# Causal attention in a three-part block: the turned softmax weights kept in two buffers, and the large tiles turned in one block at a turn's end

## The chip, the cores and the metric

The kernel runs on one core of a Trainium2 chip. The metric is the device time of one execution in microseconds, as the median of several runs. The core's engines are TensorE (PE; its weight loads are listed as PEld), VectorE (DVE), ScalarE (ACT), GpSimd (POOL) and SyncE (SP), which issues the DMA transfers of this kernel. They run side by side and wait for one another through semaphores.

## The reference

A block of three steps on x of shape (16, 512, 256), all in float32: a feed-forward step that goes by way of slots, causal self-attention with 16 heads of 64, and the feed-forward step again. Only the middle one is touched:

```
b, s, e = x.shape
q = x @ Wq + bq
kv = x @ Wkv + bkv
k, v = jnp.split(kv, [H * DQK], axis=-1)
q = _rope(q.reshape(b, s, H, DQK).transpose(0, 2, 1, 3))
k = _rope(k.reshape(b, s, H, DQK).transpose(0, 2, 1, 3))
v = v.reshape(b, s, H, DV).transpose(0, 2, 1, 3)
scores = jnp.einsum('bhqd,bhkd->bhqk', q, k) * (1.0 / np.sqrt(DQK))
causal = jnp.tril(jnp.ones((s, s), dtype=bool))
scores = jnp.where(causal[None, None], scores, -jnp.inf)
probs = jax.nn.softmax(scores, axis=-1)
out = jnp.einsum('bhqk,bhkd->bqhd', probs, v)
out = out.transpose(0, 2, 1, 3).reshape(b, s, H * DV)
return out @ Wo + bo
```

Here b = 16, s = 512, e = 256, H = 16, DQK = DV = 64; the input of this step is the layer-normalized x, and its result is added to x.

## The kernel before

The attention step is one loop. A unit is a batch and a group of four heads (HG = 4, NHG = 4 groups), so there are 16 x 4 = 64 units, and one turn of the loop works on several units at once: for u it makes the sums of unit u, turns the weights of unit u+1 (`old`), makes the scores of unit u+2 (`new`) and the queries and keys of unit u+3. The order on every engine is the order in which the program is written (manual schedule), SP's queue included.

A unit's scores are a lower triangle of 4 x 4 blocks of 128 x 128 for each head. Tile i holds the queries i*128 to i*128+127, and its keys reach as far as block i: i+1 blocks. The steps for one unit:

- `scores` (L1029): TensorE multiplies queries and keys, two contraction halves of 32 rows, four heads in different row groups of the array, into a PSUM bank per head. Tiles 3 and 2 have four banks each, tiles 1 and 0 share four. There are eight banks in all, taken in rotation.
- `exps`: VectorE scales, masks and takes the row's least value in one custom instruction (L1047), ScalarE makes the exponential and its row sum (L1051). They land in `pr0` (tiles 3 and 2: seven blocks a head) and `pr1` (tiles 1 and 0: three blocks).
- `scaled`: VectorE takes the reciprocal of the row sums (L1056), GpSimd multiplies every row (L1059).
- The sums need keys on the partitions, so every 128 x 128 block has to be turned. `turn` (L1074) is VectorE's transposition within 32 x 32 squares, from pr into `sq`; `turn_most(j)` turns six of the seven blocks of a head of pr0, `turn_corner` the seventh of all four heads, `turn_tile(1)` two blocks of all heads of pr1, `turn_tile(0)` the last one. `move` (L1101) then takes the squares to their places with 16 DMA transfers from sq into `prT`, each of 32 partitions; SP issues them.
- `sums` (L1132): TensorE multiplies the turned weights by the values, for each of two pairs of heads and each key block t over the n = 4 - t tiles that see it, the two heads of a pair in different column groups. ScalarE takes the result out and adds the bias (L1139, into `oT`).
- `leave` (L1148): TensorE's output projection; VectorE adds it to x (L1154), and at a batch's last group the rows are stored (L1156).

There is one sq and one prT (tiles in a pool with one buffer each). In the turn for u VectorE turns the first head of unit u+2 at the end (`turn_most(0)`), after the scores of tiles 1 and 0; the rest of it comes one turn later, after the exponentials of tiles 1 and 0, when the unit is `old`.

Once for each batch, layer-normalized activations also go by way of memory: `Trip` turns squares on VectorE and stores them (`away`, L947), and `land` brings them back in two halves of eight transfers each (`ahT`, L953), one half in each of the two turns that follow. In SP's order a turn is: land's eight transfers if there are any, the move, then away and the two stores of out if there are any.

The first unit and the last one are turned by TensorE instead (`turn_at_once`, L1114). The order around the change, in one turn:

```
                elif old:
                    old.scaled((1, 0), slice(0, HG // 2))
                    old.turn_most(1)
                    old.turn_most(2)
                    old.scaled((1, 0), slice(HG // 2, HG))
                    old.turn_most(3)
                    old.turn_corner()
                    old.turn_tile(1)
                if new:
                    new.scores((3,))
                    new.scores((2,))
                    new.exps((3,), slice(0, 1))
                if old and 0 <= u < nu - 2:
                    old.turn_tile(0)
                    old.move()
```

Of the kernel before, what the change touches and what calls it, by code (L numbers as in the profile page):

```python
# [9 lines left out]
F32 = mybir.dt.float32  # L10
# [24 lines left out]
HG = 4  # L35
# [12 lines left out]
def macaron_kernel(ctx: ExitStack, tc: tile.TileContext, a: dict, out: bass.AP):  # L48
# [840 lines left out]
    def attention(qp, wq, wk, wv, wo, cos, sin, row):  # L889
# [111 lines left out]
        blocks = NT * (NT + 1) // 2  # L1001
        first = [0, 4, 8, 7]
        place = {0: (1, 0, 1), 1: (1, 1, 2), 2: (0, 0, 3), 3: (0, 3, 4)}

        class Weights:
# [3 lines left out]
            def __init__(self, u):  # L1009
# [4 lines left out]
                self.pr = [None, None]  # L1014
# [47 lines left out]
            def turn(self, which, heads, of, src, dst):  # L1062
# [3 lines left out]
                if heads[0] == 0 and which == 0 and len(of) == 2:  # L1066
                    self.sq = ap.tile([P, NSQ, HG, blocks * SQ], F32, tag="sq", name=f"sq{self.nm}")
                pr = self.pr[which]

                def view(x, at, dims):  # L1070
                    return bass.AP(x.tensor, x.offset + at, [list(x.ap[0])] + [[s, n] for s, n in dims if n > 1])
                j, nh = heads
                step = (7, 3)[which] * P
                nc.vector.transpose(  # L1074
                    view(self.sq, j * blocks * SQ + dst[0] * SQ,
                         [(blocks * SQ, nh)] + [(s * SQ, n) for s, (_, n) in zip(dst[1:], of)]
                         + [(HG * blocks * SQ, NSQ), (1, SQ)]),
# [3 lines left out]
            def turn_most(self, j):  # L1081
                self.turn(0, (j, 1), [(3, 2), (1, 3)], 0, (2, 1, 3))

            def turn_corner(self):
                self.turn(0, (0, HG), [], 6, (first[3],))

            def turn_tile(self, i):
                if i:
                    self.turn(1, (0, HG), [(1, 2)], 1, (1, 3))
                else:  # L1090
                    self.turn(1, (0, HG), [], 0, (0,))

            def move(self):
# [3 lines left out]
                prT = prTs[self.u] = ap.tile([P, NSQ, HG, blocks * SQ], F32, tag="prT", name=f"prT{self.nm}")  # L1097
                for n in range(NSQ):
                    for k in range(NSQ):
                        q = (k + n) % NSQ  # L1100
                        nc.sync.dma_start(prT[k * SQ:(k + 1) * SQ, q, :, :], self.sq[q * SQ:(q + 1) * SQ, k, :, :])  # L1101

            def turn_at_once(self, tag, vector):


                prT = prTs[self.u] = ap.tile([P, NSQ, HG, blocks * SQ], F32, tag=tag, name=f"prT{self.nm}")
                where = {first[t] + i - t: (i, t) for i in range(NT) for t in range(i + 1)}
                per = S // P
                for g in range(HG * blocks // per):
                    pt = ps(f"p_prT{self.nm}_{g}")  # L1110
                    for n in range(per):
                        j, at = divmod(g * per + n, blocks)
                        i, t = where[at]
# [215 lines left out]
```

## Time and profile before

| | |
|---|---|
| time, median of 3 runs | 2311.39 us (2309.87 to 2312.6) |
| span of the profiled execution | 2307.9 us |
| granted TensorE clock, mean | 0.998 |
| PE, PEld busy | 98%, 63% |
| DVE, ACT, POOL busy | 76%, 49%, 46% |
| attention loop's sums (L1132), first to last start | 441.8 to 1917.4 us |
| prT<-sq transfers | 992 of 160.0 KB |

The span is the time from the first to the last instruction of one execution under the hardware profiler; the runs' time has what lies around it too. "Busy" is the time in which an engine had an instruction under way, as a share of the span. A share is a mean over stages: in four turns of the loop (1174.8 to 1267.8 us) the stretch-by-stretch view gives PE 92.88 of 93.00 us, DVE 83.69, ACT 50.53 and POOL 55.48. In lists of groups, "out<-in" names the tiles, "xN" is the number of instructions (a float32 product counts as two), then busy time in us, mean ns of one, and the idle time before the group with what ended it. The time of an SP row is that of issuing transfers, not of moving the data.

### The profile page before, as it was taken

What the parts mean: (1) busy time and instruction counts of PE and PEld (TensorE: products, weight loads), DVE (VectorE), ACT (ScalarE), POOL (GpSimd) and SP (SyncE); (2) the same over time, 40 slices, a digit from 0 to 9 for tenths busy, and PEclk for the clock granted to TensorE, in tenths of its full rate; (3) what the DMA queues carried; (4) which work ended last, traced back from release to release, by engine and by line L of the source; (5) the groups of instructions that cost most, each with busy time, mean ns of one, the idle gap of its engine ahead of it and who ended that gap; (6) DMA issues with size and microseconds to landing.
All of it is one profiled execution on the core that took longest, in us unless ns stands there. A gap on an engine that the chain in (4) does not pass through costs nothing. (4 is left out here: it accounts for less than half of the span.)

```text
span 2307.9 us, 42376 instructions
## 1 busy us (share of the span) xinstructions
PE 2253.5 (98%) x14424; PEld 1445.6 (63%) x14424; DVE 1761.7 (76%) x4678; ACT 1122.4 (49%) x3040; POOL 1068.0 (46%) x1692
## 2 busy tenths in 40 slices
PE   7999999999999999999999999999999999998999
PEld 5664588566656556566666665555666666764588
DVE  6742398889889898889898988988888875532387
ACT  6743243555454555455454545455545455542233
POOL 2210053555656566565655565656656552210043
PEclk9999999999999999999999999999999999999999
DMA  7839851145546465555555554646555553839834
GB/s 237 243 129 407 319 138 52 30 109 133 142 105 158 96 158 121 130 131 120 137 132 125 129 142 108 157 97 154 125 127 134 119 120 112 238 127 406 315 117 140
DMA packets 221888, 358.85 MB, mean 155 GB/s; under 512 B 99877, under 2 KB 159849, under 8 KB 213481
## 3 DMA queue, kind: packets, MB, share of 16 engines
q1 hardware_dynamic: 220812, 355.34, 55.9%
q8 instruction: 115, 1.88, 0.3%
q14 instruction: 101, 0.82, 0.1%
q10 hardware_dynamic: 860, 0.81, 0.1%
HBM read 156.29 MB, written 37.22 MB: 84 GB/s over the span
## 5 line engine op out<-in xcount | busy, mean ns | idle before, releaser
L1059 POOL TENSOR_SCALAR pr<-pr,ars 128x512 f32<-128x512 f32 (+3 forms) x1024 | 524.1, 532 | 577.5 <-DVE ars L1056 576.0
L1051 ACT ACTIVATE pr<-pr,amn 128x512 f32<-128x512 f32 (+3 forms) x1024 | 561.6, 550 | 257.4 <-DVE amn L1047 252.9
L1074 DVE STREAM_TRANSPOSE sq<-pr 128x768 f32<-128x768 f32 x434 | 384.6, 918 | 131.4 <-DMA prT<-sq 94.5
L1047 DVE CUSTOM_DVE_ANT_0 pr<-p_as,causal 128x512 f32<-128x512 f32 (+3 forms) x1024 | 433.9, 480 | 8.4 <-PE p_as L1029 7.5
L1029 PE MATMUL p_as<-k,q 32*128 32x512 f32 (+3 forms) x4096 | 315.3, 441 | 0.8 <-ACT aoT L1139 0.8
L996 ACT COPY v<-p_v 128x512 f32<-128x512 f32 x128 | 74.8, 586 | 451.2 <-PE p_v L993 451.2
L1132 PE MATMUL p_av<-prT,v 128*64 128x512 f32 (+3 forms) x2048 | 289.8, 435 | 4.2 <-ACT pr L1051 2.2
L1029 PEld LDWEIGHTS p_as<-k,q 32*128 32x128 f32 x4096 | 188.7, 185 | 108.9 <-issue 74.1
L1148 PE MATMUL p_ay<-wo,aoT 128*128 128x256 f32 x1024 | 240.1, 387 | 11.3 <-DVE amn L1047 9.8
L1148 PEld LDWEIGHTS p_ay<-wo,aoT 128*128 128x128 f32 x1024 | 190.3, 191 | 73.5 <-DVE amn L1047 49.2
L993 PE MATMUL p_v<-wv,ahT 128*128 128x256 f32 x1024 | 231.6, 379 | 0.7 <-DVE x L1154 0.7
L1132 PEld LDWEIGHTS p_av<-prT,v 128*64 128x64 f32 x2048 | 139.6, 137 | 147.6 <-issue 110.7
L971 PE MATMUL p_q<-ahT,wq 128*128 128x512 f32 x512 | 230.6, 593 | 0.2 <-ACT ahT L932 0.2
L971 PE MATMUL p_k<-ahT,wk 128*128 128x512 f32 x512 | 230.3, 592 | 0.0
L993 PEld LDWEIGHTS p_v<-wv,ahT 128*128 128x128 f32 x1024 | 194.5, 190 | 53.8 <-issue 22.2
L1051 ACT ACTIVATION_READ_ACCUMULATOR pr<-pr,amn 128x1 f32 x1024 | 191.6, 187 | 0.0
L971 PEld LDWEIGHTS p_k<-ahT,wk 128*128 128x128 f32 x512 | 97.3, 190 | 122.0 <-issue 106.9
L971 PEld LDWEIGHTS p_q<-ahT,wq 128*128 128x128 f32 x512 | 97.0, 190 | 95.7 <-issue 76.3
L762 POOL TENSOR_TENSOR kbd<-kT,own 128x256 f32<-128x256 f32 x32 | 19.7, 619 | 272.0 <-DVE kT L720 240.4
L815 PE MATMUL p_cy<-vw,catT 128*128 128x256 f32 x512 | 120.8, 379 | 0.0
L588 PE MATMUL p_ds<-hT,qk 128*128 128x512 f32 x256 | 116.0, 596 | 2.1 <-ACT hT L159 2.1
L403 PE MATMUL p_cq<-hT,c_Wq 128*128 128x512 f32 x256 | 115.1, 592 | 0.0
(174 smaller groups left out, 3206.8 us busy)
## 6 DMA issues: line engine op xcount, KB each, us to landing
prT<-sq SPq DMA_DIRECT2D x992, 160.0 KB
w<-in_e_W_dram SPq DMA_DIRECT2D x64, 1024.0 KB
w<-in_e_Wg_dram SPq DMA_DIRECT2D x32, 1024.0 KB
out_dram<-x SPq DMA_DIRECT2D x64, 256.0 KB
awaya<-sqa SPq DMA_DIRECT2D x25, 512.0 KB
atT<-awaya SPq DMA_DIRECT2D x100, 128.0 KB
xl<-in_attn_x_dram SPq DMA_DIRECT2D x16, 512.0 KB
xl<-out_dram SPq DMA_DIRECT2D x16, 512.0 KB
```

Source lines behind the costliest of these rows:

```text
L403: nc.tensor.matmul(pq, w["c_Wq"][:, k, c * P:(c + 1) * P], hTs[b][:, k, :], start=(k == 0), stop=(k == NC - 1))
L588: nc.tensor.matmul(psc, qk[:, k, c * P:(c + 1) * P], hT[:, k, :], start=(k == 0), stop=(k == NC - 1))
L815: nc.tensor.matmul(py[:, t * D:(t + 1) * D], atT[:, c, t * P:(t + 1) * P], vws[b][:, c, :], start=(c == 0), stop=(c == NC - 1))
L971: nc.tensor.matmul(pq, self.w[:, k, at:at + P], hTs[self.b][:, k, :], start=(k == 0), stop=(k == NC - 1))
L993: nc.tensor.matmul(pv[:, t * 256:(t + 1) * 256], hTs[b][:, k, (t0 + t) * P:(t0 + t + 1) * P], wv[:, k, hg * HG * DQ:(hg + 1) * HG * DQ], s ...
L1029: nc.tensor.matmul(banks[j][:, at:at + w], q[n][j * 32:(j + 1) * 32, i * P:(i + 1) * P], k[n][j * 32:(j + 1) * 32, :w], start=(n == 0), st ...
L1047: nc.vector.tensor_tensor_reduce(out=self.at(i, j), in0=banks[j][:, at:at + w], in1=causal[:, S - w:], scale=-1.0 / math.sqrt(DQ), scalar= ...
L1051: nc.scalar.activation(self.at(i, j), self.at(i, j), AF.Exp, bias=self.mn[:, i, j:j + 1], scale=-1.0, accum_out=self.rs[:, i, j:j + 1])
L1059: nc.gpsimd.tensor_scalar(self.at(i, j), self.at(i, j), self.rs[:, i, j:j + 1], 1.0, ALU.mult, ALU.mult)
L1074: nc.vector.transpose(view(self.sq, j * blocks * SQ + dst[0] * SQ, [(blocks * SQ, nh)] + [(s * SQ, n) for s, (_, n) in zip(dst[1:], of)] + ...
L1132: nc.tensor.matmul(po[j * DQ:(j + 1) * DQ, :].rearrange("d (a f) -> d a f", a=NSQ)[:, :, t * SQ:], vs[u][:, t, head * DQ:(head + 1) * DQ], ...
L1148: nc.tensor.matmul(py[:, t * D:(t + 1) * D], oTs[u][:, pair, (t0 + t) * P:(t0 + t + 1) * P], wo[:, hg * (HG // 2) + pair, :], start=(pair ...
```

## The change

Tiles 3 and 2 (index 0) and tiles 1 and 0 (index 1) now have buffers of their own: sq0 and prT0 with seven blocks a head, sq1 and prT1 with three. `where` lists the order of the blocks in each. A move has become two: `move(0)` stands at the start of a turn, `move(1)` after the small tiles have been turned, and each issues 16 transfers, of 112 KB and of 48 KB. All five transpositions of pr0 now stand at the end of the turn in which the unit is `new`, behind the scores of tiles 1 and 0 and ahead of their exponentials; the two of pr1 stay in the next turn, behind the exponentials of two heads of tile 3. `sums` runs over six pieces a pair instead of four, first four from prT0 and then two from prT1: (key block, first tile, tiles) are (0, 2, 2), (1, 2, 2), (2, 2, 2), (3, 3, 1), then (0, 0, 2), (1, 1, 1). `turn_at_once` fills both buffers. The scores and the exponentials are made as before.

```diff
--- before.py
+++ after.py
@@ -998,9 +998,11 @@
 
 
 
-        blocks = NT * (NT + 1) // 2
-        first = [0, 4, 8, 7]
+        blocks = (7, 3)
         place = {0: (1, 0, 1), 1: (1, 1, 2), 2: (0, 0, 3), 3: (0, 3, 4)}
+
+        where = ([(2, 0), (3, 0), (2, 1), (3, 1), (2, 2), (3, 2), (3, 3)], [(0, 0), (1, 0), (1, 1)])
+        pieces = [(0, t, max(t, 2), NT - max(t, 2)) for t in range(NT)] + [(1, t, t, 2 - t) for t in range(2)]
 
         class Weights:
 
@@ -1011,7 +1013,7 @@
                 self.u, self.hg, self.nm = u, hg, f"{b}_{hg}"
                 self.mn = small.tile([P, NT, HG], F32, tag="amn", name=f"amn{self.nm}")
                 self.rs = small.tile([P, NT, HG], F32, tag="ars", name=f"ars{self.nm}")
-                self.pr = [None, None]
+                self.pr, self.sq = [None, None], [None, None]
                 self.banks = {}
 
             def at(self, i, j):
@@ -1063,77 +1065,87 @@
 
 
 
-                if heads[0] == 0 and which == 0 and len(of) == 2:
-                    self.sq = ap.tile([P, NSQ, HG, blocks * SQ], F32, tag="sq", name=f"sq{self.nm}")
-                pr = self.pr[which]
+                n = blocks[which] * SQ
+                if self.sq[which] is None:
+                    self.sq[which] = ap.tile([P, NSQ, HG, n], F32, tag=f"sq{which}", name=f"sq{which}_{self.nm}")
+                pr, sq = self.pr[which], self.sq[which]
 
                 def view(x, at, dims):
                     return bass.AP(x.tensor, x.offset + at, [list(x.ap[0])] + [[s, n] for s, n in dims if n > 1])
                 j, nh = heads
-                step = (7, 3)[which] * P
+                step = blocks[which] * P
                 nc.vector.transpose(
-                    view(self.sq, j * blocks * SQ + dst[0] * SQ,
-                         [(blocks * SQ, nh)] + [(s * SQ, n) for s, (_, n) in zip(dst[1:], of)]
-                         + [(HG * blocks * SQ, NSQ), (1, SQ)]),
+                    view(sq, j * n + dst[0] * SQ,
+                         [(n, nh)] + [(s * SQ, m) for s, (_, m) in zip(dst[1:], of)]
+                         + [(HG * n, NSQ), (1, SQ)]),
                     view(pr, j * step + src * P,
                          [(step, nh)] + [(s * P, n) for s, n in of] + [(SQ, NSQ), (1, SQ)]))
 
             def turn_most(self, j):
-                self.turn(0, (j, 1), [(3, 2), (1, 3)], 0, (2, 1, 3))
+                self.turn(0, (j, 1), [(3, 2), (1, 3)], 0, (0, 1, 2))
 
             def turn_corner(self):
-                self.turn(0, (0, HG), [], 6, (first[3],))
+                self.turn(0, (0, HG), [], 6, (6,))
 
             def turn_tile(self, i):
                 if i:
-                    self.turn(1, (0, HG), [(1, 2)], 1, (1, 3))
+                    self.turn(1, (0, HG), [(1, 2)], 1, (1, 1))
                 else:
                     self.turn(1, (0, HG), [], 0, (0,))
 
-            def move(self):
-
-
-
-                prT = prTs[self.u] = ap.tile([P, NSQ, HG, blocks * SQ], F32, tag="prT", name=f"prT{self.nm}")
+            def targets(self, tag, which):
+                if which == 0:
+                    prTs[self.u] = [None, None]
+                n = blocks[which] * SQ
+                prT = prTs[self.u][which] = ap.tile([P, NSQ, HG, n], F32, tag=f"{tag}{which}",
+                                                    name=f"prT{which}_{self.nm}")
+                return prT
+
+            def move(self, which):
+
+
+
+                prT, sq = self.targets("prT", which), self.sq[which]
                 for n in range(NSQ):
                     for k in range(NSQ):
                         q = (k + n) % NSQ
-                        nc.sync.dma_start(prT[k * SQ:(k + 1) * SQ, q, :, :], self.sq[q * SQ:(q + 1) * SQ, k, :, :])
+                        nc.sync.dma_start(prT[k * SQ:(k + 1) * SQ, q, :, :], sq[q * SQ:(q + 1) * SQ, k, :, :])
 
...
         def sums(u, pair):
             b, hg = units[u]
             if pair == 0:
                 oTs[u] = ap.tile([P, HG // 2, S], F32, tag="oT", name=f"aoT{b}_{hg}")
             po = ps(f"p_av{b}_{hg}_{pair}")
-            for t in range(NT):
-                n = NT - t
+            for one, (which, t, i, n) in enumerate(pieces):
+                at = where[which].index((i, t))
                 for j in range(2):
                     head = pair * 2 + j
                     nc.tensor.matmul(
-                        po[j * DQ:(j + 1) * DQ, :].rearrange("d (a f) -> d a f", a=NSQ)[:, :, t * SQ:],
+                        po[j * DQ:(j + 1) * DQ, :].rearrange("d (a f) -> d a f", a=NSQ)[:, :, i * SQ:(i + n) * SQ],
                         vs[u][:, t, head * DQ:(head + 1) * DQ],
-                        prTs[u][:, :, head, first[t] * SQ:(first[t] + n) * SQ],
-                        start=(t == 0), stop=(t == NT - 1))
+                        prTs[u][which][:, :, head, at * SQ:(at + n) * SQ],
+                        start=(one == 0), stop=(one == len(pieces) - 1))
 
             r = R_BV + hg * (HG // 2) + pair
             nc.scalar.activation(oTs[u][:, pair, :].rearrange("d (i a y) -> d a i y", i=NT, a=NSQ),
@@ -1206,22 +1218,17 @@
                     values(0, 2)
                     old.turn_at_once("prT", range(2, 10, 3))
                 elif old:
+                    old.move(0)
                     old.scaled((1, 0), slice(0, HG // 2))
-                    old.turn_most(1)
-                    old.turn_most(2)
                     old.scaled((1, 0), slice(HG // 2, HG))
-                    old.turn_most(3)
-                    old.turn_corner()
-                    old.turn_tile(1)
                 if new:
                     new.scores((3,))
                     new.scores((2,))
-                    new.exps((3,), slice(0, 1))
+                    new.exps((3,), slice(0, 2))
                 if old and 0 <= u < nu - 2:
+                    old.turn_tile(1)
                     old.turn_tile(0)
-                    old.move()
-                if new:
-                    new.exps((3,), slice(1, 2))
+                    old.move(1)
                 gone = [leave(u, 0)] if u >= 0 else []
                 if fresh == 1:
                     width(1)
@@ -1268,7 +1275,9 @@
                 if new and u > -2:
                     new.scores((1, 0))
                     if u + 3 < nu:
-                        new.turn_most(0)
+                        for j in range(HG):
+                            new.turn_most(j)
+                        new.turn_corner()
                     new.exps((1, 0))
             token_stats(NB - 2, NT - 1)
         yield
```

Not shown in it is `turn_at_once`, whose loop over blocks now runs once for each of the two buffers.

More of the change, by code (lines that the diff above doesn't have):

```diff
@@ L1100, in move @@
                         q = (k + n) % NSQ
-                        nc.sync.dma_start(prT[k * SQ:(k + 1) * SQ, q, :, :], self.sq[q * SQ:(q + 1) * SQ, k, :, :])
+                        nc.sync.dma_start(prT[k * SQ:(k + 1) * SQ, q, :, :], sq[q * SQ:(q + 1) * SQ, k, :, :])
             def turn_at_once(self, tag, vector):
-                prT = prTs[self.u] = ap.tile([P, NSQ, HG, blocks * SQ], F32, tag=tag, name=f"prT{self.nm}")
-                where = {first[t] + i - t: (i, t) for i in range(NT) for t in range(i + 1)}
@@ L1108, in turn_at_once @@
[L1108 to L1113, printed above, removed]
-                        nc.tensor.transpose(pt[:, n * P:(n + 1) * P], self.at(i, j)[:, t * P:(t + 1) * P], ident)
-                    dst = prT.rearrange("p a h f -> p a (h f)")[:, :, g * per * SQ:(g + 1) * per * SQ]
-                    dst = dst.rearrange("p a (n x) -> p a n x", n=per)
-                    src = pt.rearrange("p (n a x) -> p a n x", n=per, a=NSQ)
-                    if g in vector:
-                        nc.vector.tensor_copy(dst, src)
-                    else:
-                        nc.scalar.copy(dst, src)
+                per, done = S // P, 0
@@ new lines, in turn_at_once @@
+                for which in range(2):
+                    prT = self.targets(tag, which)
+                    for g in range(HG * blocks[which] // per):
+                        pt = ps(f"p_prT{self.nm}_{done}")
+                        for n in range(per):
+                            j, at = divmod(g * per + n, blocks[which])
+                            i, t = where[which][at]
+                            nc.tensor.transpose(pt[:, n * P:(n + 1) * P], self.at(i, j)[:, t * P:(t + 1) * P], ident)
+                        dst = prT.rearrange("p a h f -> p a (h f)")[:, :, g * per * SQ:(g + 1) * per * SQ]
+                        dst = dst.rearrange("p a (n x) -> p a n x", n=per)
+                        src = pt.rearrange("p (n a x) -> p a n x", n=per, a=NSQ)
+                        if done in vector:
+                            nc.vector.tensor_copy(dst, src)
+                        else:
+                            nc.scalar.copy(dst, src)
+                        done += 1
```

## The prediction, made before the run

> **What bounds the kernel now.** I read the busy shares first, then the order of time on TensorE, then the transfer queue (SP's issues), then who waits for whom.
>
> ```profile
> PE 2253.5 (98%) x14424; PEld 1445.6 (63%) x14424; DVE 1761.7 (76%) x4678; ACT 1122.4 (49%) x3040; POOL 1068.0 (46%) x1692
> ```
>
> TensorE is busy for 98% of the span: an edit gains at most what is idle, and loses by every wait it puts on TensorE. Next one turn of the attention loop (one head group) on TensorE; columns are start, length, instructions:
>
> ```profile
> 1219.80 1.59 PE L1029 MATMUL p_as<-k,q 32*128 32x256 f32 x32
> 1221.32 4.53 PE L1132 MATMUL p_av<-prT,v 128*64 128x512 f32 x32
> 1225.78 3.29 PE L1029 MATMUL p_as<-k,q 32*128 32x512 f32 x32
> 1229.09 3.72 PE L1148 MATMUL p_ay<-wo,aoT 128*128 128x256 f32 x16
> ```
>
> L1132 starts at 1198.05 and at 1221.32: a turn lasts 23.26 us, as do most; the 61 turns from the second L1132 (469.8) to the last but one (1900.7) take 1430.9, or 23.46 each. TensorE has no gap; the turned weights (prT) are there in time. How narrowly, the SP issues of the same turn show:
>
> ```profile
> 1193.34 0.53 SPq L947 DMA_DIRECT2D away<-ahT  x1
> 1193.98 1.57 SPq L1156 DMA_DIRECT2D out_dram<-x  x2
> 1198.10 5.09 SPq L953 DMA_DIRECT2D ahT<-away  x8
> 1206.46 10.06 SPq L1101 DMA_DIRECT2D prT<-sq  x16
> 1216.57 4.07 SPq L953 DMA_DIRECT2D ahT<-away  x8
> ```
>
> 16 issues of a move hold SP for 10.06 us. The trace's semaphore events put the landing of the last, issued at 1215.93, at 1220.28: 1.0 us before L1132. VectorE waits for that landing too, as the moves read the one sq it turns into:
>
> ```profile
> 1217.49 0.75 DVE L977 SCALAR_TENSOR_TENSOR k<-p_k,bcol,cos 128x512 f32<-128x512 f32 x1
> 1220.41 0.98 DVE L1074 STREAM_TRANSPOSE sq<-pr 128x768 f32<-128x768 f32 x1 [2.17 <-DMA ahT<-away]
> ```
>
> (The wait is put down to the transfer that landed last; the buffer turned into is sq.) In all, VectorE waits for moves 94.5 us. TensorE's waits in the loop are small; the largest is 9.8 us:
>
> ```profile
> L1148 PE MATMUL p_ay<-wo,aoT 128*128 128x256 f32 x1024 | 240.1, 387 | 11.3 <-DVE amn L1047 9.8 <-ACT aoT L1139 0.2
> ```
>
> **The change, part by part.** *Two buffers instead of one, two moves instead of one.* The bytes stay, 2.62 MB a turn (16 x 160 KB before, 16 x 112 KB and 16 x 48 KB after). The issues double: 32 a turn. An issue costs, by its own line and by the cheapest comparable one:
>
> ```profile
> L1101 SPq DMA_DIRECT2D prT<-sq x992: 507/590/1567, 453.3 to 1896.1; - x199
> L574 SPq DMA_DIRECT2D awaya<-sqa x25: 337/338/355, 51.7 to 2045.4; - x25
> ```
>
> Start to start it is (10.06 - 0.59) / 15 = 0.631 us. Does it shrink with the bytes? The nearest rows are bound from both sides: 0.338 + 0.045 (the gap between issues) = 0.38, and 0.65. I take 0.631: it is the same line, with the same 32 rows from and to on-chip memory, and bytes do not move other rows (the 4096-byte rows of L574 take 0.338, the 8192-byte rows of the weight loads at L331 0.341 at least; the second issue of a move already takes 0.59, when nothing can be backed up).
>
> So SP issues for 32 x 0.631 = 20.2 of 23.26 us, and what decides is when it may begin. move(0) may not overwrite prT0 before the last of its readers: the fourth of six pieces of the second pair of heads. And the next turn's L1132 can't pass its fifth piece in the first pair before all of move(1) has landed. Around that loop:
>
> - TensorE after the landing: prT0 holds 7 of 10 blocks, so of a pair's 4.53 / 2 = 2.27 us its four pieces take 1.59 and prT1's two 0.68. Rest of the first pair 0.68, four pieces of the second 1.59, matmul tail and semaphore steps 0.3 (an estimate: a 128-column L1132 record lasts 0.27): 2.55.
> - first issue of move(0) to the last of move(1): 31 x 0.631 = 19.6. The two join without a gap, since move(1)'s squares are turned some 9 us into the turn and its issues begin at 14.
> - landing of the last: the first transfer of a move, with an empty queue, lands 2.46 us after issue with 160 KB; a 32 KB landing of ahT 1.64 at least. For 48 KB 1.9 (between 1.64 and 2.46).
>
> Sum 24.1 us a turn against 23.26. So in every turn TensorE waits some 0.8 us inside L1132, a wait that isn't there now.
>
> *What else is in SP's queue.* Eight ahT landings stand ahead of move(0) in two of every four turns. They take 3.8 to 4.1 us. From the last issue of move(1) SP is free after 0.64 and would be needed again after 1.9 + 2.55 = 4.45; 0.64 + 4.0 is 0.2 too long: 24.3. In one of these two, away and two stores of out come first, and the landings wait for away: 512 KB took 4.7 behind a full queue, and 2.9 (median) at L574 without one. 0.64 + 2.95 + 3.85 = 7.45, 3.0 too late: 27.1. There are 14 such groups.
>
> *Sum.* The first turn (28.0 us) has its own reasons. Of the other 61: 14 x 27.1 + 14 x 24.3 + 33 x 24.1 = 1514.9, less 1430.9: **+84 us**. The profiled span of 2307.9 becomes 2392; the runs' median is 3.5 above that span (2311.4), so 2395.
>
> *The large turns in one block at the turn's end.* No turn is added or dropped (L1074: per turn four of 0.87, pitch, and one each of 0.63, 1.2 and 0.65). The block of five takes 4.1 us from the last rope product (20.2 us into the turn), and the exponentials of tiles 1 and 0 queue behind it: they begin at 24.3, 1.05 into the next turn, instead of 0.13. ScalarE's eight then end at 5.1 to 5.5 instead of 4.15, and behind them on ScalarE the evictions of L1139 at 6.2 to 6.65 instead of 5.4. Their banks are wanted by the third and fourth head of tile 2's scores at 6.2: up to 0.5 us late for one head, some 0.25 for L1148 behind it. In return L1047 is earlier, so L1148 does not wait for it. Under the longer turn this lies in the slack; without it, it costs up to 61 x 0.25 = 15 us, and the vanished wait gives back at most 9.8. I put 0 into the sum. VectorE no longer waits for sq (2.17 above): it isn't what TensorE waits for, so nothing comes of that.
>
> *Six pieces of L1132 instead of four.* Columns stay 1280 a pair; 1024 more matmul instructions and weight loads. The shortest pieces already flow in pairs every 0.109 us, which is their share of columns at the rate of the long ones (512 in 0.429), so loads are hidden:
>
> ```profile
> L1132 PE MATMUL p_av<-prT,v 128*64 128x128 f32 x512 | 50.1, 273 | 0.0
> ```
>
> Taken: 0. The other end: five semaphore instructions of 0.107 before the fifth piece, 0.5 a turn, which the wait covers; without that wait, up to 31 us. What is queued behind this wait on TensorE is everything: scores, L1148, the next projections.
>
> *A rule against this forecast.* The Trainium skill, "DMA: Bandwidth & Descriptors" (Issuing engines are not separate DMA queues), says a sequencer's time to start a transfer is usually small beside the transfer. Here the rows say 0.631 to issue against about 0.75 us per 160 KB of data landing in a move, so they are of a size; by the rule only bytes would count, they are the same, and the sum would be 0.
>
> **The rivals.** (A) As above, 2395, **70%**. (B) Smaller pieces issue faster (0.53 or less): the loop is 2.55 + 31 x 0.53 + 1.9 = 20.9, the away turn 23.9 as today, and the moves hide. What is left is the block's 0.25: 2326; **12%**. For it: awaya's 0.338. Against: the same line's 0.590. (C) Faster: with issues that short, early release of sq and an L1047 that is earlier smooth the loop; every turn takes 23.26 (12.0 us less over 61) and L1148's 9.8 goes: 2290. It decides from a pitch of 0.53 down and only if the ScalarE evictions aren't late; **8%**. (D) Like A, but all at the upper ends: pitch 0.65, landing 2.4, away 3.75 late: 25.1, 25.3 and 28.85 make 1586, +155: 2467; **10%** for this side.
>
> **How the numbers follow.** The likeliest is A, 2395. Its own range is the pitch: 0.60 gives a loop of 23.05, hidden but for the away turn (26.05), 14 x 26.05 + 47 x 23.4 = 1465, +34, 2345; D's 2467 is the far end, of which I take half, 2430. As B and C hold 20%, I reach down to 2335. About 0.2% (5 us) is what a measurement can tell from no change. Slower: A, D and most of B, 0.87; same 0.05; faster 0.08.
>
> **What would show it.** Right: 32 issues of the move line a turn at 0.63 us, SP without rest; L1132 stretched from 4.53 to 5.3 or more, its idle time put down to prT's transfers; turns of 24.1, every fourth near 27; VectorE's wait for sq gone. Wrong: an issue of 0.45 or less, or L1132 still 4.53 long. If the turn is longer but L1132 isn't, the block on VectorE is the cause and my sum was right by luck.

## The result: the time and the profile after

The changed kernel takes 2486.12 us (median of 4 runs, 2484.55 to 2491.22) against 2310.64 us before (4 runs on the same chip, 2309.87 to 2312.6): a ratio of 1.0762, 95% interval 1.0746 to 1.0777. That is 175 us slower. The forecast said 2395 us, slower, with a range to 2430: the direction held, the size did not. The profiled execution's span went from 2307.9 to 2482.8 us.

The page of the changed kernel, busy shares first, then the groups that answer to those shown of before (busy us, mean ns, then idle time before the group and what ended it). The sums are now L1144, the turns L1077, the move L1112:

```profile
PE 2306.6 (93%) x15448; PEld 1548.0 (62%) x15448; DVE 1762.2 (71%) x4678; ACT 1127.0 (45%) x3040; POOL 1068.5 (43%) x1692
...
L1144 PE MATMUL p_av<-prT,v 128*64 128x256 f32 (+1 forms) x3072 | 343.7, 379 | 135.5 <-DMA prT<-sq 129.2
...
L1077 DVE STREAM_TRANSPOSE sq<-pr 128x768 f32<-128x768 f32 x434 | 370.4, 908 | 0.3 <-DMA prT<-sq 0.2
...
L1160 PE MATMUL p_ay<-wo,aoT 128*128 128x256 f32 x1024 | 238.6, 386 | 0.2 <-ACT aoT L1151 0.2
```

TensorE was 98% busy and is 93% busy now. The new idle time, 135.5 us, stands before the sums and is put down to the transfers of the turned weights. VectorE's wait for those transfers (94.5 us before) is gone, and so is the output projection's wait of 9.8 us: the two things that the change does free, and neither was what TensorE was waiting for.

SP's queue over four turns (start, length, instructions); this is the view that says why:

```profile
1212.19 73.10 SPq L1112 DMA_DIRECT2D prT<-sq  x96
1285.40 0.54 SPq L947 DMA_DIRECT2D away<-ahT  x1
1286.04 1.25 SPq L1168 DMA_DIRECT2D out_dram<-x  x2
1288.39 3.80 SPq L953 DMA_DIRECT2D ahT<-away  x8
1292.30 21.12 SPq L1112 DMA_DIRECT2D prT<-sq  x32
1313.46 4.04 SPq L953 DMA_DIRECT2D ahT<-away  x8
```

32 issues hold SP for some 21 us of a turn, where 16 took 10.06. (The first row holds the moves of three turns, with SP's waits between them: in all SP waits 144.3 us for TensorE to be done with prT0.) And each issue costs what it cost before; its line, durations as least, median and greatest in ns:

```profile
L1112 SPq DMA_DIRECT2D prT<-sq x1984: 507/590/2090, 449.7 to 2070.7; - x199
```

Last, TensorE around the sums in the turn behind that queue, and in the turn after it (the bracket is idle time before the row):

```profile
1308.82 1.73 PE L1144 MATMUL p_av<-prT,v 128*64 128x256 f32 x16
1314.91 5.81 PE L1144 MATMUL p_av<-prT,v 128*64 128x256 f32 x32 [4.36 <-DMA prT<-sq]
1320.66 3.29 PE L1031 MATMUL p_as<-k,q 32*128 32x512 f32 x32
...
1339.37 1.73 PE L1144 MATMUL p_av<-prT,v 128*64 128x256 f32 x16
1341.26 3.03 PE L1144 MATMUL p_av<-prT,v 128*64 128x256 f32 x32 [0.16 <-DMA prT<-sq]
```

Both times TensorE stops at the same place, before the fifth of six pieces in the first pair of heads, the first piece that reads prT1. But the 32 products behind the stop take 3.03 us in one turn and 5.81 in the other. A table by stretch gives the granted clock (the number ahead of the DMA share) for the four stretches 1303.0 to 1308.7 (before the stop), 1310.6 to 1314.9 (the stop), and the two halves of the 5.81 us:

```profile
1303.00:1308.70 5.70, 5.70 (x51) 4.49 (x49) 5.70 (x8) 1.17 (x2) 5.01 (x4) 1.00 0.43 105
1310.60:1314.90 4.30, 0.00 (x0) 0.02 (x1) 2.35 (x18) 3.61 (x16) 1.80 (x5) 0.88 0.28 71
1314.90:1317.80 2.90, 2.88 (x16) 2.05 (x18) 0.00 (x0) 0.69 (x1) 1.45 (x4) 0.50 0.43 67
1317.80:1320.70 2.90, 2.90 (x22) 1.79 (x18) 0.00 (x0) 0.00 (x0) 0.00 (x0) 0.50 0.20 35
```

The clock falls to 0.50 in the stop and stays there until it is granted again behind the sums. So the time goes in two parts. Over all turns the stops at the fifth piece are 135.5 us; in 18 of them the products behind take 4.6 to 5.8 us instead of 3.03, 39.3 us in all. Less the 9.8 us that the output projection no longer waits: 165.0. The 61 turns from the second start of the sums to the last but one take 1595.6 us against 1431.0, which is 164.6 more. That the two agree so closely is luck: the last stop and the slow products behind it, 6.6 us, lie behind these 61 turns, so the account is good to some 6 us. (The other 10 us of span lie outside these 61 turns.)

By a turn's place among four the lengths are 25.14, 29.66, 24.65 and 24.95 us, against 23.4 to 23.5 for each before.

### The profile page after: what moved, and what is told of

It is laid out like the page before. It is cut to its first block, busy times and chain, and to the rows that moved or that the text cites. A ratio compares the mean times of both kernels' runs of the same rounds, so it can differ in the third digit from the quotient of the medians.

```text
span 2482.8 us, 45849 instructions
## 1 busy us (share of the span) xinstructions
PE 2306.6 (93%) x15448; PEld 1548.0 (62%) x15448; DVE 1762.2 (71%) x4678; ACT 1127.0 (45%) x3040; POOL 1068.5 (43%) x1692
## 5 line engine op out<-in xcount | busy, mean ns | idle before, releaser
L1144 PE MATMUL p_av<-prT,v 128*64 128x256 f32 (+1 forms) x3072 | 343.7, 379 | 135.5 <-DMA prT<-sq 129.2
L1144 PEld LDWEIGHTS p_av<-prT,v 128*64 128x64 f32 x3072 | 239.3, 150 | 232.2 <-issue 130.9
L1077 DVE STREAM_TRANSPOSE sq<-pr 128x768 f32<-128x768 f32 x434 | 370.4, 908 | 0.3 <-DMA prT<-sq 0.2
L993 PEld LDWEIGHTS p_v<-wv,ahT 128*128 128x128 f32 x1024 | 194.6, 190 | 54.2 <-issue 23.4
L1151 ACT ACTIVATE aoT<-p_av,bcol 128x512 f32<-128x512 f32 x128 | 84.0, 676 | 104.6 <-PE p_av L1144 104.5
L1058 DVE RECIPROCAL ars<-ars 128x4 f32<-128x4 f32 x254 | 44.9, 177 | 118.6 <-ACT pr L1053 106.8
```

Of the source, the lines that this page charges most:

```text
L993: nc.tensor.matmul(pv[:, t * 256:(t + 1) * 256], hTs[b][:, k, (t0 + t) * P:(t0 + t + 1) * P], wv[:, k, hg * HG * DQ:(hg + 1) * HG * DQ], s ...
L1077: nc.vector.transpose(view(sq, j * n + dst[0] * SQ, [(n, nh)] + [(s * SQ, m) for s, (_, m) in zip(dst[1:], of)] + [(HG * n, NSQ), (1, SQ)] ...
L1144: nc.tensor.matmul(po[j * DQ:(j + 1) * DQ, :].rearrange("d (a f) -> d a f", a=NSQ)[:, :, i * SQ:(i + n) * SQ], vs[u][:, t, head * DQ:(head ...
L1151: nc.scalar.activation(oTs[u][:, pair, :].rearrange("d (i a y) -> d a i y", i=NT, a=NSQ), po.rearrange("d (a i y) -> d a i y", i=NT, a=NSQ ...
```

## The experiments

Two theories stood after the result. One: SP's 32 issues a turn set the loop, and the missing 80 us are in the terms of that sum. The other: the bytes, the block of large turns on VectorE or the six pieces do it. The kernels below undo or double one part each (e1, e4, e5, e6), take one found delay away (e2, e3, e7), and then look for a version of the changed kernel without its loss (e8 to e12).

**e1_half_on_act.** Half of the second move issued by ScalarE; everything else stays:

```diff
...
-                    old.move(1)
+                    old.move(1, range(2))
...
                     new.exps((2,), halfway=lambda: new.scaled((3,)))
+                if old and 0 <= u < nu - 2:
+                    old.move(1, range(2, 4), nc.scalar)
```

> Eight of move(1)'s sixteen transfers are issued from ScalarE's queue, behind the exponentials of tile 2; bytes, buffers and the order of VectorE stay. Theory (SP's issues set the turn): SP issues 24 instead of 32, its loop falls by 8 x 0.63 = 5 us, under TensorE's own 23.3 us, the wait inside L1144 goes, and the time comes back to 2300 to 2335 us. Rival 1 (the block of large turns on VectorE lengthens the turn): no change, about 2486. Rival 2 (the data, not the issues: the same bytes have to land): no change, about 2486.

Measured: 2349.25 us, ratio 1.0164 [1.015, 1.0178]; 137 of the 175 us come back with the same bytes, block and pieces. The waits of TensorE in the attention loop:

```profile
PE p_av L1143 <- DMA prT<-sq: 13.8, 17, 1.6
PE p_av L1143 <- issue: 2.8, 4, 0.9
```

The columns are us, times, longest: 129.2 us became 13.8, and no product behind a wait is slow any more. The result is 14 us over the expected band: a turn still takes 24.03 us, of which 0.4 is inside the sums (4.97 us long on the mean instead of 4.53). The issue loop is the main cause.

**e4_before_split.** The opposite test, on the kernel before: the same 2.62 MB a turn in twice the transfers, by heads:

```diff
-                        nc.sync.dma_start(prT[k * SQ:(k + 1) * SQ, q, :, :], self.sq[q * SQ:(q + 1) * SQ, k, :, :])
+                        for h in (0, HG // 2):
+                            nc.sync.dma_start(prT[k * SQ:(k + 1) * SQ, q, h:h + HG // 2, :],
+                                              self.sq[q * SQ:(q + 1) * SQ, k, h:h + HG // 2, :])
```

> The kernel before with each of the move's 16 transfers cut in two by heads (32 transfers of 80 KB, same bytes, same buffers, same order of everything else). Theory (an issue costs 0.63 us whatever its bytes, and 32 of them behind the small tiles' turns don't fit in a turn): the move lasts 8.4 + 20.3 + 2.2 us from the start of the sums, a turn of 30.9 us, or 32.8 with slow products behind a wait of 7 us: 2765 to 2880 us. Rival (bytes count, issuing is small): 2311.

Measured: 2823.29 us, ratio 1.2215 [1.219, 1.2239]. One turn on SP and on TensorE:

```profile
1217.34 20.14 SPq L1102 DMA_DIRECT2D prT<-sq  x32
```

```profile
1198.93 1.59 PE L1029 MATMUL p_as<-k,q 32*128 32x256 f32 x32
1207.38 6.19 PE L1134 MATMUL p_av<-prT,v 128*64 128x512 f32 x32 [6.87 <-DMA prT<-sq]
```

32 issues of 80 KB take 20.14 us, like 32 of 112 and 48 KB: about (20.14 - 0.59) / 31 = 0.631 from start to start in every size tried. Here the sums wait whole, as there is only one prT, and after 6.87 us of idle time they take 6.19 us instead of 4.53. So doubling the issues costs 512 us with one buffer. In the changed kernel, which has two and a first move that starts earlier in the turn, it costs 175 us, about a third of that.

**e5_before_six.** The sums of the kernel before cut into the changed kernel's six pieces:

```diff
+        pieces = [(t, max(t, 2), NT - max(t, 2)) for t in range(NT)] + [(t, t, 2 - t) for t in range(2)]
...
-            for t in range(NT):
-                n = NT - t
+            for one, (t, i, n) in enumerate(pieces):
+                at = first[t] + i - t
...
```

> The kernel before with the sums in six pieces a pair instead of four, from its one prT; nothing else changes. Prediction's step: the weight loads are hidden, 0 us, 2311 (2308 to 2314). Rival (1024 more weight loads show): up to 0.24 us a turn, +15 us, 2326.

Measured: 2313.92 us, ratio 1.0003 [0.9994, 1.0012], the sums 4.55 us long instead of 4.53:

```profile
1223.28 4.55 PE L1133 MATMUL p_av<-prT,v 128*64 128x256 f32 x48
```

1024 more products cost nothing that can be measured.

**e6_block_undone.** The changed kernel, with the large turns back in their old places in the turn (the first head at a turn's end, three heads and the corner after the exponentials of tiles 1 and 0):

```diff
-                    old.move(0)
                     old.scaled((1, 0), slice(0, HG // 2))
+                    old.turn_most(1)
+                    old.turn_most(2)
                     old.scaled((1, 0), slice(HG // 2, HG))
+                    old.turn_most(3)
+                    old.turn_corner()
+                    old.move(0)
...
-                        for j in range(HG):
-                            new.turn_most(j)
-                        new.turn_corner()
+                        new.turn_most(0)
```

> The changed kernel with the large turns back in their old places (the first head at the turn's end, the rest and the corner one turn later, and move(0) behind the corner); two buffers and two moves stay. Theory (SP's 32 issues): move(0) may begin when prT0's readers are done, 5.9 us into a turn as it is now, and the corner is turned at about 5.9 too: no change, 2486, at most +15. Rival (the block on VectorE lengthens the turn): back to about 2311.

Measured: 2509.51 us, ratio 1.0856 [1.0838, 1.0874]. The block isn't why the changed kernel is slow; without it the first move starts later (on the mean 8.3 us after the sums' start instead of 7.6), the waits are 155.3 us instead of 135.5, and slow products stand behind 27 of them instead of 18. At 23 us this is a little over the expected 15.

**e2_filler.** Is TensorE slow behind a long stop because it stood idle? In the turns that hold the long stops, eight product instructions are put in front of the fifth piece. They write into the bank of the second pair of heads, which its own first product then overwrites:

```diff
...
+                if one == 4 and pair == 0 and u % NHG == 1 and NHG < u < nu - NHG:
+                    for _ in range(4):
+                        nc.tensor.matmul(pos[u][1], wq[:, 0, 0:P], wq[:, 0, 0:S], start=True, stop=True)
```

> In every fourth turn, the one whose wait inside L1144 is 4 to 6 us long, TensorE makes four extra products of 512 columns (3.4 us) while it waits; nothing else changes. Theory (after a wait of over 4 us TensorE runs at half speed for some microseconds, so the 3.0 us of products behind the wait take 5.8): 14 turns become 2.8 us shorter, -39 us, about 2447. Rival (the products behind the wait are slow because their data or banks come late): no change, 2486, or more by what the extra products push.

Measured: 2479.18 us, ratio 1.0721 [1.0705, 1.0736]: 7 us less, not 39. The turn itself did what was expected. On TensorE, then the table by stretch for the filler and for the products behind it:

```profile
1313.18 1.74 PE L1150 MATMUL p_av<-prT,v 128*64 128x256 f32 x16
1314.84 3.70 PE L1147 MATMUL p_av<-wq 128*128 128x512 f32 x8
1318.47 3.04 PE L1150 MATMUL p_av<-prT,v 128*64 128x256 f32 x32
```

```profile
1314.80:1318.40 3.60, 3.60 (x11) 1.44 (x8) 2.32 (x17) 3.24 (x15) 1.07 (x3) 1.00 0.29 66
1318.40:1321.40 3.00, 3.00 (x33) 2.07 (x32) 0.18 (x1) 1.06 (x3) 2.18 (x6) 1.00 0.42 66
```

With TensorE kept at work the clock is 1.00 throughout and the 32 products take 3.04 us: the half rate came from the stop. The long turn falls from 29.66 to 27.71 us, but the three others rise to 25.4 to 25.8. All over, the slow products fall from 39.3 to 18.0 us and the waits (the filler's time counted in) rise from 135.5 to 148.0. Most of the 39 us expected was given back: what one turn gains, the next one waits, as long as SP's loop is the longer one.

**e3_land_on_act** and **e7_land_on_pool.** Eight of the sixteen ahT landings leave SP, for ScalarE's queue behind the exponentials of tile 2 (e3) or for GpSimd's behind the scaling of tiles 1 and 0 (e7, whose lines are shown):

```diff
...
-                if u + 4 in trips:
-                    trips[u + 4].land((0, 1))
...
                     old.scaled((1, 0), slice(HG // 2, HG))
+                if u + 4 in trips:
+                    trips[u + 4].land((0, 1), nc.gpsimd)
```

> The first half of ahT's landings (8 transfers, once in four turns) is issued from ScalarE's queue later in the same turn instead of ahead of move(0) on SP. Theory (these landings wait for away in SP's queue and hold up move(0)): the 30.6 us turn becomes an ordinary one of 24.8, 14 x 5.8 = -81 us, about 2405. Rival (that turn is long because of VectorE's turning of the activations): no change, 2486.

> As e3_land_on_act, but the first half of ahT's landings is issued from GpSimd's queue, behind the scaling of tiles 1 and 0, where it waits for nothing that SP issues in the same turn. Theory (away's landing and eight issues ahead of move(0) make the long turn): the 30.6 us turns become ordinary ones of 24.8 us, and the slow products behind the 5 us wait go with them: 14 x 5.8 = -81 us, about 2405. Rival (another cause for the long turn, say VectorE's turning of the activations): no change, 2486.

Measured: e3 2477.34 us, ratio 1.0717 [1.0703, 1.0732], a miss: the long turn only fell to 29.22 us. A part of that the trace shows: SP's moves now wait for the landings that ScalarE issues, some 2.5 us in each long turn, as the transfers of both queues use the same eight semaphores.

```profile
SPq L1112 <- DMA ahT<-away: 37.4, 15, 3.4
```

e7 2436.52 us, 1.0554 [1.053, 1.0578]. There the long turn is gone (25.04 us), as expected, with 50 of the 81 us: the others now take 25.1 to 25.8, since 32 issues a turn still set the loop. In the turn shown above, the stop and the products behind it are now:

```profile
1311.36 1.73 PE L1144 MATMUL p_av<-prT,v 128*64 128x256 f32 x16
1314.79 3.03 PE L1144 MATMUL p_av<-prT,v 128*64 128x256 f32 x32 [1.70 <-DMA prT<-sq]
```

A stop of 1.70 us leaves the products at 3.03. In eleven other turns of e7, though, stops of 1.95 to 3.89 us still make them 4.5 to 4.7, 18.2 us in all.

**e8_alternate** and **e9_pool.** Can the changed kernel be brought below the kernel before by taking eight issues of the second move off SP? SP and a second queue take turns by four transfers; the second queue is ScalarE's in e8 and GpSimd's in e9:

```diff
                 for n in range(NSQ):
+                    queue = other if other and n % 2 else nc.sync
                     for k in range(NSQ):
                         q = (k + n) % NSQ
-                        nc.sync.dma_start(prT[k * SQ:(k + 1) * SQ, q, :, :], sq[q * SQ:(q + 1) * SQ, k, :, :])
+                        queue.dma_start(prT[k * SQ:(k + 1) * SQ, q, :, :], sq[q * SQ:(q + 1) * SQ, k, :, :])
...
```

> As e1_half_on_act, but SP and ScalarE take turns by four transfers, so that none waits for a transfer that the other queue has not issued yet. Theory: with SP's 24 issues hidden and no such coupling, L1144 is 4.5 us long in nearly every turn; the time is 2300 to 2326: 2290 to 2300 if the earlier exponentials of tile 3 help TensorE (the prediction's case C), 2311 to 2326 if the block of turns costs 0 to 0.25 us a turn (case B). Rival (ScalarE has no room for 8 issues): 2340 or more, with waits for ScalarE's results on TensorE.

> As e8_alternate, with GpSimd in ScalarE's place, issuing right behind the turns of tiles 1 and 0. Theory: SP's loop is hidden again; if a GpSimd issue costs about 1 us the scaling of tile 3 starts some 6 us later and stays inside the turn: 2300 to 2345. If an issue costs far more, VectorE's block waits for the scaled tiles: over 2345.

Measured: e8 2345.22 us, ratio 1.0152 [1.0138, 1.0165]; e9 2379.81 us, 1.0301 [1.0287, 1.0315]. Neither reaches 2311, and both lie outside their theory's band: e8 in its rival's, but without the waits for ScalarE's results on TensorE that the rival named, e9 over 2345, though an issue on GpSimd costs only 0.50 us. In e8 the two queues hold each other up; SP's longest waits, and ScalarE's wait at its next work behind the issues:

```profile
SPq L1110 <- DMA prT<-sq: 207.9, 184, 5.0
```

```profile
ACT v L996 <- DMA prT<-sq: 210.3, 34, 7.1
```

SP had no such wait in the changed kernel. In e9 the sums don't wait at all, 4.55 us in every turn, and yet a turn takes 24.49 us. The scores behind the sums had become the place:

```profile
1236.30 4.55 PE L1142 MATMUL p_av<-prT,v 128*64 128x256 f32 x48
1240.78 3.60 PE L1031 MATMUL p_as<-k,q 32*128 32x512 f32 x20
1245.87 2.13 PE L1031 MATMUL p_as<-k,q 32*128 32x384 f32 x12 [1.49 <-ACT aoT L1149]
```

They wait for ScalarE's evictions of the sums, in the chain that the prediction had priced for the block with its cover gone. But the block starts late here. VectorE's last products for the rotated keys stand ahead of it, and they now wait for GpSimd's sums for the rotated queries, which stand behind the eight issues:

```profile
DVE k L977 <- POOL q L982: 55.8, 49, 3.9
DVE k L977 <- POOL q L983: 25.6, 58, 0.5
```

In e8, with the block in the same place and no issue on GpSimd, VectorE has no such wait, and the time from the end of the sums to the first output product is 3.48 us instead of e9's 4.38 (3.39 before). So e9's loss is the block and GpSimd's lateness together. That asked for one more pair.

**e10_pool_block_behind** and **e11_pool_four_behind.** e9 with the block of large turns behind the exponentials of tiles 1 and 0; and the same with four instead of eight transfers on GpSimd:

```diff
+                    new.exps((1, 0))
                     if u + 3 < nu:
                         for j in range(HG):
                             new.turn_most(j)
                         new.turn_corner()
-                    new.exps((1, 0))
```

> With half of move(1) on GpSimd's queue (e9) the sums no longer wait for the transfers (4.55 us long in every turn), and yet a turn takes 24.49 us against 23.46 before. What is left is 1.03 us a turn in the scores behind the sums (from the end of the sums to the first output product 4.35 us against 3.37 before), which wait for ScalarE's evictions of the sums: these stand behind the exponentials of tiles 1 and 0, which stand behind the block of five large turns on VectorE. Theory: this is the price of the block with its cover gone (taken as 0.25 us a turn, up to 15 us, in the prediction). Here the block goes behind exps((1, 0)); nothing else differs from e9. Then the scores flow in 3.3 us, a turn takes 23.3 to 23.6 us and the kernel 2300 to 2325. Rival: the evictions are late because GpSimd's eight issues delay its sums for the rotated queries and keys, and VectorE and ScalarE behind them; then the block's place matters little, and the time stays at 2365 to 2385.

> As e10, with only four of the sixteen transfers of move(1) on GpSimd: 28 issues for SP, 27 x 0.635 = 17.1 us and some 0.7 of slow ones from first to last. move(0) starts about 4.5 us into the turn, so the last lands at 4.5 + 17.8 + 1.9 = 24.2, and the fifth piece needs it at 23.3 + 1.6 = 24.9: hidden in ordinary turns, about 1 us late in the 14 with away and landings. Theory of the issue loop: 2305 to 2340, a little over e10 by those 14 turns, or equal to it where GpSimd's shorter hold gives something back. If the loop's sum is wrong by more than a microsecond a turn, the sums wait in every turn and it stays over 2350.

Measured: e10 2357.04 us, ratio 1.0207 [1.0193, 1.022], between the two expectations: moving the block gives 23 of e9's 69 us back. The scores wait no more. Their group in e9, then in e10 with the two groups that wait now:

```profile
L1031 PE MATMUL p_as<-k,q 32*128 32x512 f32 (+3 forms) x4096 | 387.5, 449 | 8.3 <-ACT aoT L1149 6.9 <-DVE amn L1049 1.4
```

```profile
L1031 PE MATMUL p_as<-k,q 32*128 32x512 f32 (+3 forms) x4096 | 318.7, 441 | 0.0
...
L1077 DVE STREAM_TRANSPOSE sq<-pr 128x768 f32<-128x768 f32 x434 | 371.0, 909 | 100.2 <-POOL pr L1061 100.2
...
L971 PE MATMUL p_q<-ahT,wq 128*128 128x512 f32 x512 | 236.9, 605 | 37.6 <-DVE amn L1049 37.3
```

The busy time of the scores falls by 69 us, as a product that waits inside a run of products is counted as busy. In their place VectorE waits 100.2 us for GpSimd's scaling before it turns tiles 1 and 0, and TensorE 37.3 us for VectorE. VectorE's order in one turn of e10 says why:

```profile
1199.58 4.15 DVE L1077 STREAM_TRANSPOSE sq<-pr 128x768 f32<-128x768 f32 x5
1203.65 0.20 DVE L1058 RECIPROCAL ars<-ars 128x4 f32<-128x4 f32 x2
...
1206.80 1.84 DVE L1077 STREAM_TRANSPOSE sq<-pr 128x1024 f32<-128x1024 f32 x2 [1.61 <-POOL pr L1061]
1208.56 0.65 DVE L1049 CUSTOM_DVE_ANT_0 pr<-p_as,causal 128x512 f32<-128x512 f32 x1
```

The block now stands ahead of the reciprocals of tiles 1 and 0, GpSimd scales behind these, the turns of those tiles wait for that, and the exponentials of the rest of tile 3 and of tile 2 come behind the turns: the block's price has moved and not gone. e11 took 2401.97 us, ratio 1.039 [1.0372, 1.0408], a miss: the sums wait 64.8 us again. The 28 issues take the 17.8 us expected, but the first move starts 6.6 us into a turn (median) and not at 4.5, as the block that fills its squares now stands behind the exponentials.

**e12_scaled_in_block.** As e10, with the reciprocals and the scaling taken into the block:

```diff
-                    old.scaled((1, 0), slice(0, HG // 2))
-                    old.scaled((1, 0), slice(HG // 2, HG))
...
-                        for j in range(HG):
-                            new.turn_most(j)
+                        new.turn_most(0)
+                        new.scaled((1, 0), slice(0, HG // 2))
+                        new.turn_most(1)
+                        new.turn_most(2)
+                        new.scaled((1, 0), slice(HG // 2, HG))
+                        new.turn_most(3)
                         new.turn_corner()
```

> In e10 the reciprocals of tiles 1 and 0 stand behind the block of large turns on VectorE; GpSimd's scaling starts behind them, the turns of these tiles wait for it (100.2 us of idle time before the turns, 1.2 in e9), and the exponentials of tile 2 and the projections behind those follow late (37.3 us of TensorE's time). Here the reciprocals go into the block, the first behind one large turn and the second behind three, and GpSimd scales from there; everything else is as in e10. Theory (the block's new place is what is left): the turns' wait and the projections' 37 us go, a turn takes 23.4 to 23.8 us and the kernel 2310 to 2330, about the kernel before. Rival (GpSimd's eight issues are what is left): the turns' wait goes or not, but the sums for the rotated queries and keys on GpSimd are late as before, and the time stays at 2345 or more.

Measured: 2309.43 us (2305.86 to 2312.63, 11 runs) against 2311.87 (15 runs of the kernel before), ratio 0.9989 [0.998, 0.9998]. On its page:

```profile
PE 2256.2 (98%) x15448; PEld 1513.1 (66%) x15448; DVE 1758.9 (76%) x4678; ACT 1124.1 (49%) x3040; POOL 1309.7 (57%) x2188
...
L1077 DVE STREAM_TRANSPOSE sq<-pr 128x768 f32<-128x768 f32 x434 | 378.5, 911 | 0.1
...
L1142 PE MATMUL p_av<-prT,v 128*64 128x256 f32 (+1 forms) x3072 | 295.1, 346 | 7.3 <-DMA ahT<-away 4.2 <-DMA prT<-sq 1.5 <-issue 1.4
L971 PE MATMUL p_q<-ahT,wq 128*128 128x512 f32 x512 | 230.6, 593 | 0.2 <-ACT ahT L932 0.2
```

Both waits of e10 are gone, TensorE is at 98% again, and a turn takes 23.43 us against 23.46. The theory holds, 0.6 us below its band: e9's 69 us were what stands ahead of what on VectorE and GpSimd, not GpSimd's issues as such. VectorE waits for GpSimd's sums as it did in e9 (92.7 us in all); with the block out from behind that wait it costs nothing. The whole of the change (two buffers, 32 transfers, six pieces, a block) fits into the old time, once eight issues leave SP and the block is in nobody's way. It is lower than the kernel before by 2.4 us, 0.1%, less than what the prediction counts as a difference: in the loop of the kernel before TensorE stood still for 0.12 of 93 us, so there was that little to gain.

## Why the prediction was right and wrong

**The issue's price: right.** It stays at 0.59 us and 0.045 between two, for 112 and for 48 KB; e4 shows the same for 80 KB. The choice between 0.38 and 0.65 went to the right end, and so rivals B and C, which needed shorter issues, fell. Bytes alone, the reading by the Trainium skill's "DMA: Bandwidth & Descriptors" (Issuing engines are not separate DMA queues), would have made it 0; in these runs the time to start the transfers is what sets the loop.

**The loop: right in its three links, short in size.** From the first issue of move(0) to the next turn's first, worked out from the trace's issues and semaphore events for 60 loops, mean us, forecast in brackets:

| loops | first to last issue | landing of the last | landing to next move(0) | together |
|---|---|---|---|---|
| nothing else ahead on SP (31) | 20.25 (19.6) | 1.97 (1.9) | 2.74 (2.55) | 24.97 (24.1) |
| eight landings ahead (15) | 20.40 (19.6) | 1.93 (1.9) | 4.50 (2.8) | 26.82 (24.3) |
| away, out and landings ahead (14) | 20.24 (19.6) | 2.12 (1.9) | 6.07 (5.6) | 28.43 (27.1) |

**The step that failed** is the sum itself, at "first issue of move(0) to the last of move(1): 31 x 0.631 = 19.6" and at "0.64 + 4.0 is 0.2 too long: 24.3". Two terms were left out of it.

- *Slow issues.* 53 of the 1984 issues take over 0.65 us, up to 2.09, together 41.2 us above the median: some 0.65 us a turn, which is the difference between 19.6 and 20.3. The row quoted in the prediction had it: its greatest was 1567 ns beside a median of 590. I took the pitch from one undisturbed move; the mean over all moves of the kernel before is 0.645. Before, 23 of 992 issues were slow, 12.8 us, and were hidden.
- *The clock behind a long stop.* In the loop behind an away turn TensorE stops for 4 to 6 us and then works at half its rate: 4.50 instead of 2.8 in the second row of the table. e2 shows the half rate to be the stop's doing, e7 that it goes in that turn when the long stop goes.

Weighed over the 60 loops, the first column accounts for 0.68 x 60 = 41 us, the landing for 6, the last link for 0.19 x 31 + 1.7 x 15 + 0.47 x 14 = 38: together 85, against the 81 that lie between the forecast's 84 and the 164.6 measured in 61 turns. Some 12 of the 85 are neither of the two terms: the landing, and the link of the away turns at 6.07 instead of 5.6.

**Which turns: right in kind.** "Every fourth near 27" is every fourth at 29.66, by the two terms above. One sign did not show, "SP without rest": SP waits 144.3 us in its loop, for TensorE to be done with prT0. The sum itself had that wait in it.

**The block at nothing: right under the longer turn; what it costs uncovered stays open.** In e6 its absence costs 23 us: the earlier first move is worth more than assumed. For the block without cover the prediction had 0.25 us a turn, 15 us at most. In e9 the chain that it named (exponentials, evictions, banks, scores) costs some 70 us, but it was priced with every other engine on time: the exponentials of tiles 1 and 0 begin 2.0 us into the turn and not at 1.05, behind VectorE's wait for GpSimd. In e8, with GpSimd free, the scores lose only 0.09 us a turn, but there the sums are 0.4 us longer and cover a part. What the prediction missed is that the scaling behind the block belongs to the chain too (e10). The block's price alone was not measured.

**Six pieces at nothing: right** (e5). **VectorE's wait for sq gone, worth nothing: right**; 131.4 us of idle time before the turns became 0.3.

**The range** ended at half of rival D's surplus. D, pitch and landing at their upper ends, gave 2467. The landing was at 1.97 and not at D's 2.4, but the mean pitch, slow issues counted, is 20.25 / 31 = 0.653, D's upper end. D's loops of 25.1, 25.3 and 28.85 stand beside 24.97, 26.82 and 28.43 measured. Two are near, partly by luck, as a landing that was taken too long made up for a last link that was taken too short. The middle one falls short, in the turns where the clock is halved, which no case had; by that the time lay beyond D's as well.

**What stays open.** What makes an issue slow was not tried by experiment. In the trace all 53 slow issues overlap in time with an instruction fetch (packets on queues of kind "instruction"), and 118 of the other 1931 do; in the kernel before it is 23 of 23 and 37 of 969. That is a coincidence in time, not a cause shown. Nor was the block tried with one move and two sq. Why a turn of e1 and e8 is still 24.0 us, with 17 us of stops left, is explained by the queues' waits for each other only in part. e12 moves GpSimd's scaling ahead of its other work as well as the reciprocals; which of the two does it was not separated.

## What to carry to other kernels

Count issues, not bytes, when a move is split: find the queue that issues, multiply the mean of its pitch (outliers included) by the new count, and put that into the loop that it closes with the engine that frees its buffer. When such a sum yields a stop of the matrix engine of several us, add the time that it runs at half its clock behind it. And when issues go to another engine, or work is gathered into a block, follow what is queued behind it there: here the same parts cost 69 us in one order and nothing in another.

## What the runs showed of the hardware

- **TensorE's clock after a stop.** Of 60 stops in the changed kernel, the 40 of 0.16 to 1.92 us left the 32 products behind them at 3.03 us; of the six from 1.96 to 2.69 us four made them 4.7; all fourteen of 3.92 us and more made them 4.6 to 5.8. The Trainium skill, "TensorE: Matmul & The Clock Gate" (What's actually happening), says that the clock halves after an idle window of about 3.4 us which runs freely, and comes back after a busy one; that agrees with the fourteen, while four stops here were already enough at 1.96 to 2.69 us. The length alone does not decide among the short ones: in e7 a stop of 1.95 us made the products 4.7, and one of 2.78 left them at 3.03. The trace's clock record has 18 stretches at 0.50 for these stops, six of 3.41 us and twelve of 6.83.
- **An issue from and to on-chip memory costs the same whatever its bytes**: 0.59 us for 48, 80, 112 and 160 KB, all of 32 rows.
- **A second issuing queue**: the same transfer's issue takes 0.60 us (median) on ScalarE and 0.50 on GpSimd, and what the engine has behind the issues comes later: in e9 VectorE then waits 81.4 us for GpSimd's sums. With ScalarE as the second queue SP waited 207.9 us for other transfers of the move, with GpSimd (e12) for none.
